# Attention between two sequences on one core: the steady batches and the last batch put in another order

## The chip, the cores and the metric

The kernel runs on one core of a Trainium2 chip. The metric is the device time of one execution, in microseconds (us); less is better. Five engines work side by side and wait for each other by semaphores: TensorE (PE) multiplies matrices into PSUM, VectorE (DVE) and ScalarE (ACT) read PSUM and the on-chip memory, GpSimd (POOL) works on the on-chip memory alone, SyncE (SP) starts transfers. Each engine runs its own instructions in their order.

## The reference

`x` and `y` (`ctx_2048`) are 32 batches of 256 x 1024 floats. `C` is 256 channels, `N` is 1024 columns.

```python
x_q = jnp.einsum('oc,bcn->bno', w_qk, y)
x_k = jnp.einsum('oc,bcn->bon', w_qk, x)
x_v = jnp.einsum('oc,bcn->bon', w_v, x) + b_v[None, :, None]
energy = jnp.einsum('bnc,bcm->bnm', x_q, x_k)
attention = jax.nn.softmax(energy, axis=-1)
attention = attention / (1e-07 + attention.sum(axis=1, keepdims=True))
x_r = jnp.einsum('bcn,bnm->bcm', x_v, attention)
x_r = jax.nn.relu(jnp.einsum('oc,bcn->bon', w_t, x - x_r) + b_t[None, :, None])
return x + x_r
```

So the softmax goes over the rows of the energy, and each column of the result is then divided by its own sum over the rows plus 1e-7 (`EPS`).

## The kernel before

Weights are multiplied together once at the start (`w_qk` with itself, `w_v` with `w_t`, `w_t` alone), and each float operand is split into three forms, HIGH, REST and LOW, so that three quick matmuls add up to one exact product. Six matmuls (three forms, two halves of the channels) make one result of 128 x 512.

Work goes batch by batch, `cur` being the batch in hand, `nxt` the next and `last` the one before. The 1024 rows of the energy are eight row tiles `n` of 128, the columns two halves `h` of 512, the channels two halves `c` of 128. PSUM is `banks`, eight banks used as four pairs. Pairs 0 and 1 hold the energy of two row tiles in turn (`place(n)`), and also the keys and one group of the values; pairs 2 and 3 collect the attention's result for `c` 0 and 1, and before that take the other group of values and the straight part.

The steps of a batch, by method name:

- `values(q)`: 24 matmuls with 256 columns for one group q of four row tiles; then `high` (ACT), `low` and `rest` (DVE) write its three forms. `v0`, `v1` are the two groups.
- `energy(n)`: 12 matmuls. `lowest(n)` (DVE), `exp(n)` (ACT, also the row sum), `recip(n)` (DVE). `high(n, h)` (ACT), `rest(n, h)` (DVE), `scaled(n)` (ACT) and `low(n)` (POOL) write the forms of the softmax, all four of them being `forms(n)`. `share(n)` (DVE, a step for each half) adds the row tile into `acc`, from which the column sums come.
- `straight(c)`: 12 matmuls of `w_t` with x; `straight_out(c)` (ACT) takes it from PSUM to `xe`.
- `attention(n)`: 12 matmuls into pairs 2 and 3, four pieces (c, h) of three.
- `keys(i)`: 12 matmuls for the next batch, with `high` (ACT), `low`, `rest` (DVE) as `k0`, `k1`.
- `columns()` and `inverse()` (DVE): sum `acc` over its rows and spread the reciprocals over the partitions as `rc`. `divided(c)` (DVE) reads pair 2 + c, `joined(c)` (POOL) adds `xe`, and in the next batch `relu(c)` (ACT) and `put(c)` (POOL add of x loaded again by `load_out`, then the store) finish it.
- In the last batch, `finish(c, h)` does the end by quarters: divided, a maximum, a sum, a store.

Every compute engine is wrapped in `InOrder`, so the order of its instructions is that of the calls in the program; the SP queue is ordered by the scheduler. Raw tiles of x and y share four buffers (`rawp`), the softmax forms three (`ep`). Every recorded instruction has the line of the wrapper, L66, so the profile's groups are told apart by tile names: `ef` forms of the softmax, `uf` of the values, `gf` of the keys, `xf`, `yf` of x and y, `nm`, `rs`, `ri` the smallest value of a row, the row sum and its reciprocal.

In a steady batch PE's order is values(0), energy(0), values(1), straight(0), energy(1), straight(1), energy(2), attention(0), energy(3), attention(1) and so on to energy(7), attention(5), then keys(0), attention(6), keys(1), attention(7). In the last batch there are no keys, and the pieces of attention are drawn from a list, three behind each energy:

```python
if n + 2 < NT:
    cur.energy(n + 2)
    attend(3)
```

Of the kernel before, what the change touches and what calls it, by code (L numbers as in the profile page):

```python
# [9 lines left out]
F32 = mybir.dt.float32  # L10
F32R = mybir.dt.float32r
AF = mybir.ActivationFunctionType
ALU = mybir.AluOpType
# [4 lines left out]
def kernel(  # L18
# [24 lines left out]
    FORMS = 3  # L43
    HIGH, LOW, REST = range(FORMS)
# [27 lines left out]
    load = nc.sync.dma_start  # L72
# [3 lines left out]
    def pair(j):  # L76
        return banks[:, 2 * j : 2 * j + 2]
# [4 lines left out]
    def value(v):  # L82
        return v.bitcast(F32)
# [56 lines left out]
    class Weights:  # L140
# [12 lines left out]
        def low(self):  # L153
            act.mul(self.l, self.d, UP)
# [49 lines left out]
    class Batch:  # L204
# [136 lines left out]
        def scaled(self, n):  # L341
            act.mul(self.ef[n][:, LOW], value(self.ef[n][:, HIGH]), 1.0 / UP)

        def low(self, n):
            f = self.ef[n]
            pool.tensor_tensor(f[:, LOW], value(f[:, LOW]), value(f[:, REST]), ALU.add)

        def share(self, n, halves=range(MH)):
            p, ri = self.place(n), self.row[n]
            if n == 0:  # L350
# [36 lines left out]
        def inverse(self):  # L387

            def moved(out_, in_):
                dve.tensor_reduce(out_, in_.unsqueeze(2), AX.X, ALU.add)  # L390

            s = sc[:, :, 0]
            for a in range(1, NG):
                moved(parts[:G32, :, a], parts[ts(a, G32), :, 0])
            dve.tensor_reduce(s[:G32], parts[:G32], AX.X, ALU.add)
            dve.reciprocal(s[:G32], s[:G32])
            moved(s[G32 : 2 * G32], s[:G32])
            moved(s[2 * G32 :], s[: 2 * G32])
            rc = one.tile([P, NB, G32], F32, tag="rc", name=f"rc_{self.b}")
# [23 lines left out]
        def end_sum(self, c):  # L423
            pool.tensor_tensor(self.xo[c], self.xo[c], self.xe[:, c], ALU.add)

        def end_least(self, c):
            act.mul(self.xe[:, c], self.xe[:, c], -1.0)

        def finish(self, c, h):

            if c == 0 and h == 0:
                self.z = one.tile([P, KC, N], F32, tag="z", name=f"z_{self.b}")
            at = ts(h, MB)
            p, zh, xh = pair(2 + c)[:, h], self.z[:, c, at], self.xo[c][:, at]
            final = (c, h) == (KC - 1, MH - 1)
            dve.scalar_tensor_tensor(p, p, ubias[:, c], self.rc[:, at], ALU.add, ALU.mult)
            dve.tensor_tensor(zh, p, self.xe[:, c, at], ALU.max)
            (dve if final else pool).tensor_tensor(zh, zh, xh, ALU.add)
            load(out[self.b, ts(c, P), at], zh)


    def square(into, left, right):
# [86 lines left out]
    for b in range(B - 1):  # L529
        nxt = Batch(b + 1)  # L530

        if b == 0:
            v0 = cur.values(0)
            v0.high()
            v1 = cur.values(1)
            v0.low()
            v0.rest()
            act.copy(th, wtT)
            pool.tensor_tensor(wd, wtT, value(th), ALU.subtract)
            pool.tensor_tensor(  # L540
                product, wt, bv.unsqueeze(1).to_broadcast([P, KC, C]), ALU.mult
            )
# [24 lines left out]
            for h in range(MH):  # L567
                cur.high(1, h)
                cur.rest(1, h)
            cur.straight_out(1)  # L570
            cur.scaled(1)
            cur.low(1)
        else:
            v0 = cur.values(0)
            v0.high()
            cur.energy(0)
            cur.lowest(0)
            v0.low()
# [24 lines left out]
            cur.scaled(1)  # L603
            cur.low(1)
        nxt.load_x()
        cur.energy(2)
        cur.share(1)
        for n in range(2, NT):
# [5 lines left out]
            cur.exp(n)  # L614
            cur.recip(n)
            cur.forms(n)
            cur.attention(n - 2, first_order if b + n == 2 else None)
            if n == 2:
                nxt.x_high(0)
                nxt.x_rest(0)  # L620
# [28 lines left out]
        for q in later:  # L649
# [10 lines left out]
        for c in range(KC):  # L660
            cur.divided(c)
            cur.joined(c)
        for q in later:
            ys[q].low()
        last, cur = cur, nxt


    units = [(n, c, h) for n in range(NT - 2) for c in range(KC) for h in range(MH)]

    def attend(count):  # L670
        for _ in range(count):
            n, c, h = units.pop(0)
            cur.attention(n, [(c, h)])

    v0 = cur.values(0)
    v0.high()
    cur.energy(0)
    cur.lowest(0)
    v0.low()
    v1 = cur.values(1)  # L680
    cur.exp(0)
    cur.recip(0)
    v1.high()
    v0.rest()
    cur.forms(0)
    cur.straight(0)
    cur.straight_out(0)
    last.relu(0)
    last.load_out()
    last.put(0)  # L690
    cur.share(0)
    v1.low()
    cur.energy(1)
    cur.lowest(1)
    v1.rest()
    cur.straight(1)
    cur.energy(2)
    cur.exp(1)
    cur.straight_out(1, ts(0, 1))
    cur.recip(1)  # L700
    more_ef = one.tile([P, KC, FORMS, N], F32R, tag="xf", name="more_ef")
    for n in (3, 4):
        cur.ef[n] = more_ef[:, n - 3]
    for n in range(1, NT):
        if n > 1:
            cur.exp(n)
            cur.recip(n)
        cur.high(n, 0)
        cur.share(n, [1])
        cur.rest(n, 0)  # L710
        if n == 1:
            cur.straight_out(1, ts(1, 1))
        if n + 1 < NT:
            cur.lowest(n + 1)
        cur.high(n, 1)
        cur.share(n, [0])
        cur.rest(n, 1)
        if n + 2 < NT:
            cur.energy(n + 2)
            attend(3)  # L720
        cur.scaled(n)
        cur.low(n)
        if n == 2:
            last.relu(1)
            last.put(1)
            cur.load_out()
        elif n == 4:
            cur.end_sum(0)
        elif n == 5:
            cur.end_sum(1)  # L730
    attend(len(units))
    cur.columns()
    cur.inverse()
    for c in range(KC):
        cur.end_least(c)
    for c in range(KC):
        for h in range(MH):
            for n in (NT - 2, NT - 1):
                cur.attention(n, [(c, h)])
            cur.finish(c, h)  # L740


# [28 lines left out]
```

## Time and profile before

| | |
|---|---|
| median of 3 runs | 1949.26 us (1946.62 to 1949.41) |
| profiled execution, its own time | 1947.41 us |
| its span | 1945.6 us |
| granted TensorE clock | 0.999 |
| busy: PE, DVE, ACT, POOL | 1936.5, 1555.5, 1465.2, 1257.6 us |

The span is what the trace covers, from the first to the last instruction; the execution's own time has 1.8 us more around it. In a row of the timeline stand start, duration, engine, line, operation, output<-input, shape and count, and in brackets idle time ahead of it with what ended it.

### The profile page before, as it was taken

Reading aid. Unit: us, or ns where it says so; the run is one execution under the profiler, and the core shown is the slowest. Engines: PE = TensorE matmul, PEld = TensorE weight load, DVE = VectorE, ACT = ScalarE, POOL = GpSimd, SP = SyncE. Lnnn points to the kernel's source line nnn. Section 1 sums busy time; section 2 is a strip of 40 time slices with the busy share of each in tenths; the row PEclk is TensorE's granted clock in tenths of the full one; section 3 lists DMA queues with packets and bytes.
Section 4 is the critical chain, followed back from the end, with each engine's and each line's share of the span. In section 5 each row is a group of like instructions: output and inputs, shape, how many; then the busy total and the mean of one; then the engine's idle time right before and its main releaser. Section 6 shows DMA issues by size and latency. Waiting matters only on the chain.

```text
span 1945.6 us, 25143 instructions
## 1 busy us (share of the span) xinstructions
PE 1936.5 (100%) x9246; PEld 1631.4 (84%) x9246; DVE 1555.5 (80%) x2162; ACT 1465.2 (75%) x1899; POOL 1257.6 (65%) x646
## 2 busy tenths in 40 slices
PE   9999999999999999999999999999999999999998
PEld 8888888888888888888888888888888888888886
DVE  7877788877888778887788877788777888778888
ACT  7777777777777877777877777777777777777765
POOL 5666766667657676666666666666667566676565
PEclk9999999999999999999999999999999999999999
DMA  4644546545455444555454644546445455454531
GB/s 138 152 113 118 124 111 141 123 116 130 108 130 130 120 119 113 126 132 124 113 123 116 145 114 119 119 119 141 114 118 125 110 141 123 115 131 109 130 98 44
DMA packets 81852, 235.35 MB, mean 121 GB/s; under 512 B 7488, under 2 KB 8384, under 8 KB 81728
## 3 DMA queue, kind: packets, MB, share of 16 engines
q0 software_dynamic: 35136, 98.58, 29.3%
q1 hardware_dynamic: 46448, 135.02, 20.5%
q8 instruction: 73, 1.20, 0.2%
q14 instruction: 51, 0.42, 0.1%
q10 hardware_dynamic: 144, 0.13, 0.0%
HBM read 134.61 MB, written 33.55 MB: 86 GB/s over the span
## 4 chain that ended last, share of the span: by engine, by line
PE 99%; DVE 1%; issue 0%; ACT 0%; DVEq 0%; ACTq 0%
PE banks L66 99%; DVE z L66 0%; DVE banks L66 0%; DVE nm L66 0%; DVE ef L66 0%; DVE acc L66 0%; DVE parts L66 0%; DVE rc L66 0%; DVE sc L66 0%; ACT ef L66 0%; DVE few L66 0%; DVE ri L66 0%; DVEq L66 0%; ACTq L66 0%
## 5 line engine op out<-in xcount | busy, mean ns | idle before, releaser
L66 POOL TENSOR_TENSOR ef<-ef 128x1024 fp32r<-128x1024 f32 x254 | 611.4, 2407 | 444.8 <-ACT ef L66 328.4
L66 PE MATMUL banks<-gf,yf 128*128 128x512 f32 x3072 | 739.4, 390 | 2.2 <-DVE acc L66 2.1
L66 PE MATMUL banks<-ef,uf 128*128 128x512 f32 x3048 | 731.9, 389 | 0.0
L66 PEld LDWEIGHTS banks<-gf,yf 128*128 128x128 f32 x3072 | 574.0, 188 | 122.5 <-issue 4.8
L66 PEld LDWEIGHTS banks<-ef,uf 128*128 128x128 f32 x3048 | 572.1, 188 | 118.8
L66 DVE SCALAR_TENSOR_TENSOR ef<-banks,ri,ef 128x512 fp32r<-128x512 f32 x508 | 358.4, 746 | 210.4 <-ACT ef L66 210.3
L66 ACT ACTIVATE banks<-banks,nm 128x1024 f32<-128x1024 f32 x256 | 278.0, 1086 | 275.8 <-DVE nm L66 269.8
L66 DVE TENSOR_REDUCE nm<-banks 128x1 f32<-128x1024 f32 x256 | 312.8, 1222 | 86.6 <-PE banks L66 84.9
L66 ACT ACTIVATE ef<-banks,ri 128x512 fp32r<-128x512 f32 x508 | 322.6, 687 | 54.6 <-DVE ri L66 45.3
L66 DVE SCALAR_TENSOR_TENSOR acc<-banks,ri,acc 128x512 f32<-128x512 f32 x448 | 314.3, 742 | 0.2
L66 ACT ACTIVATE ef<-ef 128x1024 fp32r<-128x1024 f32 x254 | 270.5, 1065 | 7.1
L66 POOL DMA_DIRECT2D yf<-in_ctx_dram x63 | 76.7, 1217 | 189.5 <-ACT yf L66 187.4
L66 PEld LDWEIGHTS banks<-vw,xf 128*128 128x128 f32 x1536 | 192.6, 191 | 4.9
L66 PE MATMUL banks<-vw,xf 128*128 128x256 f32 x1536 | 194.1, 283 | 0.0
L66 PE MATMUL banks<-xf,tw 128*128 128x512 f32 x768 | 185.2, 390 | 0.0
L66 PE MATMUL banks<-xf,gw 128*128 128x512 f32 x768 | 184.7, 389 | 0.0
L66 PEld LDWEIGHTS banks<-xf,gw 128*128 128x128 f32 x768 | 144.0, 188 | 29.9
L66 PEld LDWEIGHTS banks<-xf,tw 128*128 128x128 f32 x768 | 142.2, 188 | 28.2
L66 POOL TENSOR_TENSOR z<-z,xe 128x1024 f32<-128x1024 f32 x62 | 147.5, 2394 | 22.1 <-DVE z L66 22.1
L66 POOL TENSOR_TENSOR z<-z,xo 128x1024 f32<-128x1024 f32 (+1 forms) x65 | 152.1, 2340 | 3.7 <-DVE z L66 3.7
L66 POOL TENSOR_TENSOR xf<-x,xf 128x1024 fp32r<-128x1024 f32 x62 | 149.3, 2407 | 0.0
L66 ACT ACTIVATE yf<-yf 128x1024 fp32r<-128x1024 f32 x127 | 131.0, 1055 | 2.0
(72 smaller groups left out, 1314.2 us busy)
## 6 DMA issues: line engine op xcount, KB each, us to landing
x<-in_x_dram SPq DMA_DIRECT2D x64, 512.0 KB, 3.5
y<-in_ctx_dram SPq DMA_DIRECT2D x64, 512.0 KB, 4.6
xo<-in_x_dram SPq DMA_DIRECT2D x64, 512.0 KB, 3.5
yf<-in_ctx_dram POOLq DMA_DIRECT2D x63, 512.0 KB, 6.5
yf<-yf POOLq DMA_DIRECT2D x63, 512.0 KB, 5.2
xf<-xf POOLq DMA_DIRECT2D x62, 512.0 KB, 6.2
out_dram<-z SPq DMA_DIRECT2D x62, 512.0 KB, 3.0
out_dram<-z SPq DMA_DIRECT2D x4, 256.0 KB, 2.0
```

Source lines behind the costliest of these rows:

```text
L66: self.last = getattr(self.engine, name)(*args, **kwargs)
```

## The change

Four things are changed.

1. Steady batches. PE does values(0) and values(1) one behind the other, then energy(0), straight(0), energy(1), straight(1), energy(2); straight(1) goes into pair 2. On DVE the two steps of v0 and the first of v1 stand ahead of lowest(0), share(0) stands behind lowest(1). `relu(0)`, `load_out` and `put(0)` of the batch before go behind the forms of row tile 1. `attention(0)` starts with the pieces of c = 1.
2. The end of a steady batch. `divided(0)` and `joined(0)` stand ahead of k1's `low` and `rest`, `divided(1)` and `joined(1)` behind them.
3. The last batch (with the steps of the batch before that are still open) is a list of words, each one step, with halves of energies and pieces of attention as single words. The last row tile's forms are made from a copy on ACT (`end_share`, `end_high`, `end_scaled`) and two steps on POOL (`end_rest` for the first half, `low` by halves).
4. Its column sums. `EPS / P` is added in the first share; a matmul with `few`, now a matrix that adds the four groups of 32 rows (`gather_groups`, filled by POOL in batch 0), and one reciprocal stand where `inverse` had eight small steps. The first quarter of the end is divided into `z` and done by POOL and ACT.

```diff
     def share(self, n, halves=range(MH)):
...
-                    dve.tensor_scalar(a, p[:, h], ri, None, ALU.mult)
+                    if self.b < B - 1:
+                        dve.tensor_scalar(a, p[:, h], ri, None, ALU.mult)
+                    else:
+                        dve.tensor_scalar(a, p[:, h], ri, EPS / P, ALU.mult, ALU.add)
...
+        def end_group_sums(self):
+            into = self.place(NT - 2)[:, 0, :NB]
+            pe.matmul(into, few, parts[:, :, 0], start=True, stop=True)
+
+        def end_recip(self):
+            dve.reciprocal(sc[:, :, 0], self.place(NT - 2)[:, 0, :NB])
...
+        def end_share(self, h):
+            act.mul(self.sh[:, ts(h, MB)], self.place(n)[:, h], self.row[n])
+        def end_high(self, h):
+            act.copy(self.ef[n][:, HIGH, ts(h, MB)], self.sh[:, ts(h, MB)])
+        def end_scaled(self, h):
+            act.mul(f[:, LOW], value(f[:, HIGH]), 1.0 / UP)
+        def end_rest(self, h):
+            pool.tensor_tensor(f[:, REST], self.sh[:, ts(h, MB)], value(f[:, HIGH]), ALU.subtract)
...
+    def gather_groups():
+        two_groups = 2 * G32
+        pool.tensor_tensor(
+            few[:, :two_groups], ident[:, :two_groups], ident[:, two_groups:], ALU.add
+        )
+        pool.tensor_tensor(few[:, :G32], few[:, :G32], few[:, G32:two_groups], ALU.add)
+        for a in range(1, NG):
+            pool.tensor_copy(few[:, ts(a, G32)], few[:, :G32])
...
             v0 = cur.values(0)
             v0.high()
+            v1 = cur.values(1)
+            v0.low()
+            v0.rest()
             cur.energy(0)
+            v1.high()
+            v1.low()
             cur.lowest(0)
-            v0.low()
-            v1 = cur.values(1)
+            v1.rest()
+            cur.straight(0)
             cur.exp(0)
             cur.recip(0)
-            v1.high()
-            v0.rest()
-            cur.forms(0)
-            cur.straight(0)
+            cur.high(0, 0)
+            cur.rest(0, 0)
+            cur.high(0, 1)
+            cur.rest(0, 1)
             cur.straight_out(0)
-            last.relu(0)
-            last.load_out()
-            last.put(0)
-            cur.share(0)
-            v1.low()
+            cur.scaled(0)
+            cur.low(0)
             cur.energy(1)
             cur.lowest(1)
-            v1.rest()
+            cur.share(0)
             cur.exp(1)
             cur.recip(1)
-            cur.straight(1)
-            cur.straight_out(1, ts(0, 1))
+            cur.straight(1, 2)
+            last.load_out()
...
-            cur.straight_out(1, ts(1, 1))
+            cur.straight_out(1)
             cur.scaled(1)
             cur.low(1)
+            last.relu(0)
+            last.put(0)
...
-        k1.low()
-        k1.rest()
         cur.attention(NT - 1)
...
+        if nxt.b < B - 1:
+            divide(0)
+            k1.low()
+            k1.rest()
+            divide(1)
...
+    steps = """
+        V0 vh0 ylow klow krest div0 vl0 E01 join0 vr0 pos0 E00 min0 exp0 div1 V1 E11 ri0 sum01
+        vh1 h00 outx E10 vl1 h01 X0 join1 min1 exp1 lastx r01 xw0 s0 r00 sum00 ri1 put0 sum10
+        sum11 E21 h10 E20 min2 X1 r10 h11 r11 exp2 ri2 sum21 x11 h21 l0 sum20 E30 s1 E31 r21 l1
+        h20 min3 r20 A011 E41 vr1 x10 A010 exp3 ri3 E40 sum31 min4 s2 l2 A001 h30 A110 h31 r31
+        A101 r30 exp4 ri4 h40 A111 h41 E51 A210 sum30 sum40 E50 s3 xs01 pos1 r40 r41 E60 sum41
+        E61 A000 s4 min5 A201 exp5 ri5 h51 min6 A100 h50 A200 xsw1 r51 sum51 sum50 l3 A310 A300
+        exp6 E71 s5 l4 ri6 put1 h61 r50 E70 h60 r61 l5 r60 s6 min7 A211 sum61 A400 sum60 exp7
+        ri7 sh0 sum71 A410 A301 sum70 A311 eh0 sh1 A500 l6 es0 eh1 cols es1 A510 A610 er0 el0
+        A401 A501 r71 G A600 least01 A700 A710 A411 A601 inv el1 leastw1 turn d00 plus relu A701
+        d10 m10 o10 o00 d01 m01 A511 o01 A611 A711 d11 m11 o11
+    """
```

The words: V values (the digit is q), E energy (n, h), X straight (c), A attention (n, c, h), G the group matmul; vh, vl, vr high, low and rest of the values; min, exp, ri, sum (n, h), h, r, s, l the steps of a row tile; sh, eh, es, er, el the same for the last one; x, xw straight_out; cols, inv, turn the column sums, the reciprocal and its spread; d, m, o divided, maximum and out by quarters (c, h).

More of the change, by code (lines that the diff above doesn't have):

```diff
@@ L342, in scaled, with low @@
             act.mul(self.ef[n][:, LOW], value(self.ef[n][:, HIGH]), 1.0 / UP)
-        def low(self, n):
-            f = self.ef[n]
+        def low(self, n, at=slice(0, None)):
+            f = self.ef[n][:, :, at]
             pool.tensor_tensor(f[:, LOW], value(f[:, LOW]), value(f[:, REST]), ALU.add)
@@ L349, in share @@
             p, ri = self.place(n), self.row[n]
-            if n == 0:
+            if not hasattr(self, "acc"):
                 self.acc = one.tile([P, N], F32, tag="acc", name=f"acc_{self.b}")
@@ L398, in inverse, with turned @@
             moved(s[2 * G32 :], s[: 2 * G32])
+            self.turned()
+        def turned(self):
             rc = one.tile([P, NB, G32], F32, tag="rc", name=f"rc_{self.b}")
@@ L421, in put, with end_sum, end_least @@
             load(out[self.b, ts(c, P)], self.z[:, c])
[L423 to L431, printed above, removed]
+        def end_sum(self, c, at=slice(0, None)):
+            xo = self.xo[c][:, at]
+            pool.tensor_tensor(xo, xo, self.xe[:, c, at], ALU.add)
+        def end_least(self, c, at=slice(0, None)):
+            act.mul(self.xe[:, c, at], self.xe[:, c, at], -1.0)
@@ new lines, in end_share @@
+        def end_share(self, h):
+            n = NT - 1
+            if h == 0:
+                self.sh = rawp.tile([P, N], F32, tag="raw", name="share")
+            act.mul(self.sh[:, ts(h, MB)], self.place(n)[:, h], self.row[n])
+        def end_high(self, h):
+            n = NT - 1
+            if n not in self.ef:
+                self.ef[n] = ep.tile([P, FORMS, N], F32R, tag="ef", name="ef_last")
+            act.copy(self.ef[n][:, HIGH, ts(h, MB)], self.sh[:, ts(h, MB)])
+        def end_scaled(self, h):
+            f = self.ef[NT - 1][:, :, ts(h, MB)]
+            act.mul(f[:, LOW], value(f[:, HIGH]), 1.0 / UP)
@@ L432, in finish, with piece @@
+        def end_rest(self, h):
+            f = self.ef[NT - 1][:, :, ts(h, MB)]
+            pool.tensor_tensor(f[:, REST], self.sh[:, ts(h, MB)], value(f[:, HIGH]), ALU.subtract)
+        def piece(self, c, h):
+            if not hasattr(self, "z"):
                 self.z = one.tile([P, KC, N], F32, tag="z", name=f"z_{self.b}")
             at = ts(h, MB)
-            p, zh, xh = pair(2 + c)[:, h], self.z[:, c, at], self.xo[c][:, at]
-            final = (c, h) == (KC - 1, MH - 1)
-            dve.scalar_tensor_tensor(p, p, ubias[:, c], self.rc[:, at], ALU.add, ALU.mult)
@@ L437, in finish, with end_divided @@
-            dve.tensor_tensor(zh, p, self.xe[:, c, at], ALU.max)
-            (dve if final else pool).tensor_tensor(zh, zh, xh, ALU.add)
-            load(out[self.b, ts(c, P), at], zh)
+            return pair(2 + c)[:, h], self.z[:, c, at], self.xe[:, c, at], self.xo[c][:, at]
+        def end_divided(self, c, h):
+            p, zh, xe, xh = self.piece(c, h)
+            dve.scalar_tensor_tensor(
+                p if c + h else zh, p, ubias[:, c], self.rc[:, ts(h, MB)], ALU.add, ALU.mult
+            )
@@ new lines, in end_max, with end_plus, end_relu, end_out @@
+        def end_max(self, c, h):
+            p, zh, least, xh = self.piece(c, h)
+            dve.tensor_tensor(p if c == h == 1 else zh, p, least, ALU.max)
+        def end_plus(self):
+            p, zh, xe, xh = self.piece(0, 0)
+            pool.tensor_tensor(zh, zh, xe, ALU.add)
+        def end_relu(self):
+            zh = self.piece(0, 0)[1]
+            act.activation(zh, zh, AF.Relu)
+        def end_out(self, c, h):
+            p, zh, xe, xh = self.piece(c, h)
+            if c == h == 1:
+                dve.tensor_tensor(zh, p, xh, ALU.add)
+            else:
+                pool.tensor_tensor(zh, zh, xh, ALU.add)
+            load(out[self.b, ts(c, P), ts(h, MB)], zh)
@@ L616 @@
             cur.forms(n)
-            cur.attention(n - 2, first_order if b + n == 2 else None)
+            cur.attention(n - 2, first_order if n == 2 else None)
+            if b == 0 and n == 4:
+                gather_groups()
             if n == 2:
@@ L656, with divide @@
             ys[q].scaled()
-        k1.low()
-        k1.rest()
         cur.attention(NT - 1)
-        for c in range(KC):
+        def divide(c):
             cur.divided(c)
             cur.joined(c)
-        for q in later:
-            ys[q].low()
-        last, cur = cur, nxt
[L668 to L740, printed above, removed]
+        if nxt.b < B - 1:
[3 more added lines that the diff above has]
+            divide(1)
+            for q in later:
+                ys[q].low()
+        last, cur = cur, nxt
+    v = {}
+    def open_values(q):
+        v[q] = cur.values(q)
@@ new lines, in late_high @@
+    def late_high(n, h):
+        if n == 3 and n not in cur.ef:
+            more = one.tile([P, KC, FORMS, N], F32R, tag="xf", name="more_ef")
+            cur.ef[n], cur.ef[n + 1] = more[:, 0], more[:, 1]
+        cur.high(n, h)
+    steps = {
+        "klow": lambda: k1.low(),
+        "krest": lambda: k1.rest(),
+        "ylow": lambda: ys[B * MH - 1].low(),
+        "div": lambda c: last.divided(c),
+        "join": lambda c: last.joined(c),
+        "pos": lambda c: last.relu(c),
+        "lastx": lambda: last.load_out(),
+        "put": lambda c: last.put(c),
+        "V": open_values,
+        "vh": lambda q: v[q].high(),
+        "vl": lambda q: v[q].low(),
+        "vr": lambda q: v[q].rest(),
+        "X": lambda c: cur.straight(c),
+        "xw": lambda c: cur.straight_out(c),
+        "x": lambda c, h: cur.straight_out(c, ts(h, 1)),
+        "E": lambda n, h: cur.energy(n, [h]),
+        "min": lambda n: cur.lowest(n),
+        "exp": lambda n: cur.exp(n),
+        "ri": lambda n: cur.recip(n),
+        "sum": lambda n, h: cur.share(n, [h]),
+        "h": late_high,
+        "r": lambda n, h: cur.rest(n, h),
+        "s": lambda n: cur.scaled(n),
+        "l": lambda n: cur.low(n),
+        "A": lambda n, c, h: cur.attention(n, [(c, h)]),
+        "outx": lambda: cur.load_out(),
+        "xsw": lambda c: cur.end_sum(c),
+        "xs": lambda c, h: cur.end_sum(c, ts(h, MB)),
+        "leastw": lambda c: cur.end_least(c),
+        "least": lambda c, h: cur.end_least(c, ts(h, MB)),
+        "sh": lambda h: cur.end_share(h),
+        "eh": lambda h: cur.end_high(h),
+        "es": lambda h: cur.end_scaled(h),
+        "er": lambda h: cur.end_rest(h),
+        "el": lambda h: cur.low(NT - 1, ts(h, MB)),
+        "cols": lambda: cur.columns(),
+        "G": lambda: cur.end_group_sums(),
+        "inv": lambda: cur.end_recip(),
+        "turn": lambda: cur.turned(),
+        "d": lambda c, h: cur.end_divided(c, h),
+        "m": lambda c, h: cur.end_max(c, h),
+        "plus": lambda: cur.end_plus(),
+        "relu": lambda: cur.end_relu(),
+        "o": lambda c, h: cur.end_out(c, h),
+    }
@@ L744 @@
+    """
+    for word in STEPS.split():
+        name = word.rstrip("0123456789")
+        steps[name](*(int(a) for a in word[len(name):]))
 _INS = [
```

2 lines of the change are left out of this document (added).

## The prediction

> **What bounds the kernel now.** First the page: which engine fills the span, at what clock, and what the chain of work that ended last is made of.
>
> ```profile
> span 1945.6 us, 25143 instructions
> ...
> PE 1936.5 (100%) x9246; PEld 1631.4 (84%) x9246; DVE 1555.5 (80%) x2162; ACT 1465.2 (75%) x1899; POOL 1257.6 (65%) x646
> ...
> PEclk9999999999999999999999999999999999999999
> ...
> PE 99%; DVE 1%; issue 0%; ACT 0%; DVEq 0%; ACTq 0%
> ```
>
> PE is busy throughout and carries 99% of the chain, at an even clock. As the ends of matmuls are modelled, I look at starts instead, in the timeline of PE alone around the head of a steady batch.
>
> ```profile
> 975.29 2.88 PE L66 MATMUL banks<-ef,uf 128*128 128x512 f32 x12
> 978.01 3.04 PE L66 MATMUL banks<-vw,xf 128*128 128x256 f32 x24
> 980.89 2.91 PE L66 MATMUL banks<-gf,yf 128*128 128x512 f32 x12
> 983.63 3.04 PE L66 MATMUL banks<-vw,xf 128*128 128x256 f32 x24
> 986.51 2.91 PE L66 MATMUL banks<-xf,tw 128*128 128x512 f32 x12
> 989.25 2.88 PE L66 MATMUL banks<-gf,yf 128*128 128x512 f32 x12
> 994.69 2.88 PE L66 MATMUL banks<-gf,yf 128*128 128x512 f32 x12
> ```
>
> Twelve matmuls of 512 columns take 2.72 us from start to start (975.29 to 978.01; 989.25 to 994.69 is two blocks), 0.2267 each; the 24 of a group of values take 2.88. Nothing waits: a steady batch is pure PE work, and no order of other engines' work can shorten it. The only excess is 0.02 us in the block behind each group of values (980.89 to 983.63 and 986.51 to 989.25 are 2.74). So a gain has to come from the last batch, and a loss could come from any wait that the new steady order opens, thirty times over.
>
> The last batch, in the timeline from its first matmul on:
>
> ```profile
> 1881.28 3.04 PE L66 MATMUL banks<-vw,xf 128*128 128x256 f32 x24
> ...
> 1897.96 2.88 PE L66 MATMUL banks<-gf,yf 128*128 128x512 f32 x12
> 1900.88 1.23 DVE L66 TENSOR_REDUCE nm<-banks 128x1 f32<-128x1024 f32 x1 [0.95 <-PE banks L66]
> ...
> 1902.91 3.00 PE L66 MATMUL banks<-gf,yf 128*128 128x512 f32 x12 [2.07 <-DVE acc L66]
> 1905.74 2.20 PE L66 MATMUL banks<-ef,uf 128*128 128x512 f32 x9
> 1905.94 1.22 DVE L66 TENSOR_REDUCE nm<-banks 128x1 f32<-128x1024 f32 x1 [0.47 <-PE banks L66]
> ...
> 1907.09 0.74 DVE L66 SCALAR_TENSOR_TENSOR acc<-banks,ri,acc 128x512 f32<-128x512 f32 x1
> ...
> 1907.97 3.00 PE L66 MATMUL banks<-gf,yf 128*128 128x512 f32 x12
> ...
> 1923.16 2.99 PE L66 MATMUL banks<-gf,yf 128*128 128x512 f32 x12
> ...
> 1931.42 8.32 PE L66 MATMUL banks<-ef,uf 128*128 128x512 f32 x36
> ...
> 1940.41 0.75 DVE L66 SCALAR_TENSOR_TENSOR banks<-banks,ubias,rc 128x512 f32<-128x512 f32 x1
> 1941.19 0.69 DVE L66 TENSOR_TENSOR z<-banks,xe 128x512 f32<-128x512 f32 x1
> 1941.99 0.69 DVE L66 TENSOR_TENSOR z<-z,xo 128x512 f32<-128x512 f32 x1
> ```
>
> Here PE does wait. The last 36 matmuls need 36 x 0.2267 = 8.16, so PE is through at 1939.58, 58.30 us after 1881.28. Its work: up to the end of energy(2) 1897.96 + 2.72 - 1881.28 = 19.40; five more energies 13.60; eight attentions, 96 matmuls, 21.76; together 54.76. The waits are 58.30 - 54.76 = **3.54 us**: 2.23 ahead of energy(3) (1902.91 - 1900.68), which needs the first row tile of that place to be read out; about 0.30 in each of four rounds of energy and nine attention matmuls, (1923.16 - 1902.91) / 4 = 5.06 against 21 x 0.2267 = 4.76; 0.1 at the end. The 0.30 is seen in one round: energy(3) ends at 1905.63, lowest(3) starts at 1905.94, the share of tile 2 at 1907.09 lasts 0.74, and energy(4) starts at 1907.97. That is 2.34 us on DVE, covered by 9 x 0.2267 = 2.04 of PE.
>
> **Part one, the steady batches.** PE's work per batch is the same; one of two changes from values to another block goes: 30 x 0.02 = **0.6 us**. What must hold is that nothing comes late. I go through the new order on the times of the batch above (V0 is values(0) at 978.01), with these rows of DVE, ACT, SP and again ACT (and one of the groups by form, for the low and rest of the values):
>
> ```profile
> 976.61 1.25 DVE L66 STREAM_TRANSPOSE rc<-sc 128x1024 f32<-128x1024 f32 x1
> 977.78 1.18 DVE L66 SCALAR_TENSOR_TENSOR gf<-gf,banks 128x1024 fp32r<-128x1024 f32 x1
> 979.00 1.23 DVE L66 SCALAR_TENSOR_TENSOR gf<-banks,gf 128x1024 fp32r<-128x1024 f32 x1
> 980.14 2.47 DVE L66 SCALAR_TENSOR_TENSOR z<-banks,ubias,rc 128x1024 f32<-128x1024 f32 x2
> 989.67 1.40 DVE L66 TENSOR_SCALAR acc<-banks,ri 128x512 f32<-128x512 f32 x2
> ...
> L66 DVE SCALAR_TENSOR_TENSOR uf<-banks,uf 128x1024 fp32r<-128x1024 f32 x64 | 77.4, 1210 | 0.0
> ...
> 981.09 1.03 ACT L66 ACTIVATE uf<-banks 128x1024 fp32r<-128x1024 f32 x1 [0.65 <-PE banks L66]
> ...
> 995.26 13.65 SPq L167 DMA_DIRECT2D y<-in_ctx_dram  x2
> ...
> 1031.18 1.04 ACT L66 CAST yf<-y 128x1024 fp32r<-128x1024 f32 x1
> ```
>
> - V1 is now due at 978.01 + 2.88 = 980.89 and overwrites pair 2, so divided(0) must have read it. divided(0) takes the place of k1.low at 977.78 and, at 1.27 (two take 2.47), ends at 979.05: 1.8 us to spare. The two steps of k1 end at about 981.4; energy(0), which needs them, is due at 978.01 + 5.76 = 983.77. divided(1) ends at 982.6, straight(0), which overwrites pair 3, is due at 986.5.
> - v0.high ends at 982.1 as before; v0.low and v0.rest, 1.21 each, follow divided(1) and end at 985.0, energy(1) is due at 989.2. v1.high ends at 985.0, v1.low at 986.2, lowest(0) at 987.9, v1.rest at 989.1; straight(1), now into pair 2, is due at 991.95.
> - energy(2) is due at 994.67 and needs share(0), which stands behind lowest(1) now. From energy(1)'s end at 991.95: 0.2 to start, 1.15, to the next step, and 0.74 for the first half make 994.05 (the 1.15 and 0.74 are those of 1905.94 and 1907.09 above); the second half, 0.66 later as 1.40 for two has it, is needed 1.36 later. Spare 0.6, the narrowest place.
> - Of the moved steps, put(0) goes some 8 us later on POOL; its store on SP goes with it to about 1003, and the load of y behind it, issued at 995.26, waits as long. That y is first read at 1031.18: free. The order of loads and stores on SP is the same in both programs. The five small POOL steps that fill `few` lie in batch 0, ahead of two DMAs whose data the keys need only after four more blocks of 2.72: free; without that cover they cost what they last, once.
>
> So part one: -0.6, with bounds 0 and -0.6.
>
> **Part two, the last batch.** The list is laid out so that the rows above do not bind. Each place is refilled behind more PE work: between E20's end and E30 stands straight(1), 2.72; between E31 and E40 stand A011, E41 and A010, 0.68 + 1.36 + 0.68 = 2.72; between E40 and E51 stand four pieces, 2.72; all against the 2.34 that the round above needs. energy(2) has straight(0) in front of it; E60 needs tile 4's steps, which stand ahead of lowest(5) on DVE; E71 has 4.08 of pieces in front of it (from E61's end) for lowest 1.15, a rest and a share, 0.7 each. So the 3.54 should go: **-3.54**. If the 2.34 grew by 0.4 on DVE, these would wait again (a rival below). POOL has 13 steps of at most 2.41 us in the 42 us before energy(7) ends (54.8 less the nineteen pieces behind it, 12.9), 31 of 42, and stays off PE's way; its mean is in the page:
>
> ```profile
> L66 POOL TENSOR_TENSOR ef<-ef 128x1024 fp32r<-128x1024 f32 x254 | 611.4, 2407 | 444.8 <-ACT ef L66 328.4
> ```
>
>
> The end is the second place where something could come late. Two rows of DVE for it from the same timeline, then four groups of the list by form (busy us, mean ns):
>
> ```profile
> 1928.88 0.76 DVE L66 SCALAR_TENSOR_TENSOR acc<-banks,ri,acc 128x512 f32<-128x512 f32 x1
> ...
> 1931.65 1.24 DVE L66 TRANSPOSE_TENSOR_REDUCE parts<-acc 128x32 f32<-128x1024 f32 x1
> ...
> L66 ACT ACTIVATE ef<-banks,ri 128x512 fp32r<-128x512 f32 x508 | 322.6, 687 | 54.6 <-DVE ri L66 45.3 <-POOL ef L66 9.0
> ...
> L66 POOL TENSOR_TENSOR z<-z,xo 128x512 f32<-128x512 f32 x3 | 3.8, 1283 | 3.7 <-DVE z L66 3.7
> ...
> L66 PE MATMUL banks<-few 128*128 128x128 f32 x10 | 2.5, 437 | 1.1 <-DVE few L66 1.1
> ...
> L66 DVE RECIPROCAL sc<-sc 32x32 f32<-32x32 f32 x32 | 10.9, 341 | 1.1
> ```
>
> From energy(7)'s end (1925.88) to the first share of tile 7 (1928.88) it was 3.0 us; two shares, 1.4, and the column sums, 1.24, make 5.7. The group matmul stands behind ten pieces, 6.8 us: 1.1 to spare, and this matmul and one reciprocal stand where `inverse` had eight small steps of DVE. Behind it: the reciprocal (at most 0.34), the transpose 1.25, divided 0.75 twice and a maximum 0.69, with lags some 4.2, against six pieces, 4.08. They run level, and the three pieces behind (2.04) cover the 1.44 of the next divided and maximum. ACT and POOL bring the last row tile's forms: two ACT steps, 0.69 each, and two POOL steps of half size, 1.28 each, make 6.9 with the 3.0 ahead of them, due after 7.9. So PE sets the end, and the saving on DVE is worth nothing by itself.
>
> After PE's last matmul come three DVE steps in both kernels. Before, they began at 1940.41, though the matmul's modelled end is 1931.42 + 8.32 = 1939.74; a free DVE begins 0.04 behind such an end (1897.96 + 2.88 = 1900.84, and 1900.88). So 0.67 - 0.04 = **-0.63** goes there.
>
> The group matmul itself is new on PE. The five matmuls with `few` show ten records, two each, 437 ns busy. Two in sequence are 0.87, the upper bound; below, it cannot cost less than nothing, since PE must do it. I take 0.4, half of that, since those ten stand in the cold start of the kernel and move 128 columns, this one 32: **+0.4**. The Trainium skill, "FP8 and Floating Point Precision", TensorE Precision Notes, says that true FP32 takes four passes through the array; the trace shows two records for each such matmul. Four passes of that length are an estimated 1.75 and would leave a gain of 3.0.
>
> **The sum.** -3.54 - 0.63 + 0.4 - 0.6 = **-4.37 us**. The profiled execution took 1947.41 (span 1945.6 and 1.8 around it) and would take 1943.0; the three runs shown have their median at 1949.26, so I forecast **1944.9**. The runs lie between 1946.62 and 1949.41, so 0.2% (3.9 us) is about what a measurement can tell from no change, and the forecast is hardly more than that.
>
> **Rivals.**
> - *The handovers keep waiting.* With ACT and DVE both reading the same bank, or POOL late, some 0.3 stays at five of the new handovers: 1.5, so 1946.4. For it: the spare is only 0.4 at three of them. Against: the 2.34 they are held to is already a measured chain.
> - *The matmul is dear and the change of block costs nothing to begin with.* At 0.87 for the matmul and 0.3 for the values, the gain is 3.6: 1945.7. For it: 0.02 is the size of the trace's grain. Against: the steady batch is 60.2 us throughout, with that 0.02 in it.
> - *Slower: V1 waits for divided(0) in each steady batch.* It now follows V0 directly. If divided(0) ran where it did (980.14 + 1.27, and 0.14 until PE goes on, as from 1907.83 to 1907.97 above), V1 would wait 0.66 us, thirty times: 20 us, 1964.9. It decides from divided(0) ending after 980.75. For it: DVE is on the edge there, with the inverse ending just as V0 starts. Against: k1's two steps are moved behind, 1.8 to spare.
> - *The group matmul runs four records.* The rows give two for a matmul with `few`, but of another size; at four of 437 ns it takes 1.75, PE and with it the end come 1.35 later than forecast: 1946.3. The skill's sentence on four passes speaks for it, the ten records of five matmuls against it.
>
> **How the numbers follow.** Forecast 0.52, of which 0.37 beyond 0.2% and 0.15 within, as run to run differences of a us or more either side decide there; handovers 0.20 (0.05 and 0.15); dear matmul 0.13 (0.08 and 0.05); four records 0.08 (0.02 and 0.06); V1 0.07 (0.02 within, 0.05 slower). Sum: faster 0.52, same 0.43, slower 0.05. The range goes from 1942.6 (the forecast less 2.3, as far as the lowest run lies under the median) to 1947.4 (the handover case and 1 us); what is left out is V1's 0.07 and about 0.1 at the ends.
>
> **What would show it.** In the profile after: values x48 in one row of PE, followed by one block of 2.74, and a batch of 60.18 us; 54.8 to 55.3 us from the last batch's first matmul to its last with no idle time put down to DVE; two records of the group matmul; the last divided right behind the last matmul. It would be wrong if PE idles ahead of V1 or of energy(2) in every batch, or if the end is a chain of DVE from the transpose on.

## The result, and the profile after

The changed kernel took 1942.97 us (median of 11 runs, 1942.0 to 1943.72) against 1948.2 of the kernel before (11 runs, 1946.62 to 1949.41): a ratio of 0.9974, interval 0.9966 to 0.9982. The forecast was 1944.9, faster, with hardly more than 0.2%. The profiled execution took 1943.16 where that of before took 1947.41, and its span is 1941.4.

PE around the head of the steady batch that starts at 978 us, from the timeline (start, duration, count at the end):

```profile
978.28 5.92 PE L66 MATMUL banks<-vw,xf 128*128 128x256 f32 x48
984.03 2.91 PE L66 MATMUL banks<-gf,yf 128*128 128x512 f32 x12
986.78 2.88 PE L66 MATMUL banks<-xf,tw 128*128 128x512 f32 x12
989.50 2.88 PE L66 MATMUL banks<-gf,yf 128*128 128x512 f32 x12
```

Values take 5.75 us in one row, the block behind them 2.75, the next ones 2.72. Between the first values of two steady batches lie 60.18 us in place of 60.20. DVE in the same stretch:

```profile
976.87 1.25 DVE L66 STREAM_TRANSPOSE rc<-sc 128x1024 f32<-128x1024 f32 x1
978.32 1.28 DVE L66 SCALAR_TENSOR_TENSOR z<-banks,ubias,rc 128x1024 f32<-128x1024 f32 x1 [0.20 <-DVE rc L66]
...
992.42 1.22 DVE L66 TENSOR_REDUCE nm<-banks 128x1 f32<-128x1024 f32 x1 [0.56 <-PE banks L66]
993.56 1.40 DVE L66 TENSOR_SCALAR acc<-banks,ri 128x512 f32<-128x512 f32 x2
```

divided(0) ends at 979.60, 1.56 us before values(1) begins at 978.28 + 2.88 = 981.16; the first half of share(0) ends at about 994.3, energy(2) starts at 994.94. Both have the room that was worked out, less 0.2 for divided(0), which waits for the transpose (k1's step in that place did not need it).

The last batch on PE, with DVE's last steps:

```profile
1880.97 3.04 PE L66 MATMUL banks<-vw,xf 128*128 128x256 f32 x24
...
1900.38 2.88 PE L66 MATMUL banks<-gf,yf 128*128 128x512 f32 x12
1903.10 0.84 PE L66 MATMUL banks<-ef,uf 128*128 128x512 f32 x3
1903.78 1.52 PE L66 MATMUL banks<-gf,yf 128*128 128x512 f32 x6
1905.14 0.84 PE L66 MATMUL banks<-ef,uf 128*128 128x512 f32 x3
1905.82 1.52 PE L66 MATMUL banks<-gf,yf 128*128 128x512 f32 x6
...
1929.62 0.31 PE L66 MATMUL banks<-parts,few 128*128 128x32 f32 x2
1929.75 0.94 PE L66 MATMUL banks<-ef,uf 128*128 128x512 f32 x3
1930.53 1.55 PE L66 MATMUL banks<-ef_last,uf 128*128 128x512 f32 x6
1931.92 0.85 PE L66 MATMUL banks<-more_ef,uf 128*128 128x512 f32 x3
...
1935.32 0.84 PE L66 MATMUL banks<-ef_last,uf 128*128 128x512 f32 x3
```

```profile
1930.36 1.25 DVE L66 STREAM_TRANSPOSE rc<-sc 128x1024 f32<-128x1024 f32 x1
...
1934.16 0.76 DVE L66 SCALAR_TENSOR_TENSOR banks<-banks,ubias,rc 128x512 f32<-128x512 f32 x1 [0.26 <-PE banks L66]
...
1936.20 0.76 DVE L66 SCALAR_TENSOR_TENSOR banks<-banks,ubias,rc 128x512 f32<-128x512 f32 x1 [0.56 <-PE banks L66]
1936.99 0.70 DVE L66 TENSOR_TENSOR banks<-banks,xe 128x512 f32<-128x512 f32 x1
1937.73 0.69 DVE L66 TENSOR_TENSOR z<-banks,xo 128x512 f32<-128x512 f32 x1
```

No idle time stands at any row of PE. Its work ends at 1935.32 + 0.68 = 1936.00, 55.03 us after 1880.97, where before it took 58.30. The last three DVE steps begin 0.20 us behind that, where before it was 0.83 (1940.41 against 1939.58), and DVE now waits for PE in the last two quarters. The chain that ended last and PE's waits over the whole span say the same:

```profile
14 pieces in order of time: start us, us, what
...
7.38 0.14 issue
7.52 1928.66 PE banks L66 x9230
1936.18 0.03 issue
1936.20 0.77 DVE banks L66
```

```profile
PE banks L66 <- DVE parts L66: 1.1, 1, 1.1
PE banks L66 <- DMA stage<-in_L_xattn_w_t_dram: 0.9, 1, 0.9
```

One piece of PE, 1928.66 us long, with three DVE steps behind it. The two waits left lie in the first 8 us; the second, for a load, put the first values at 15.24 us, where they were at 14.70 before.

### The profile page after: what moved, and what is told of

The parts are those of the page before. It is cut to its first block, busy times and chain, and to the rows that moved or that the text cites. A ratio compares the mean times of both kernels' runs of the same rounds, so it can differ in the third digit from the quotient of the medians.

```text
span 1941.4 us, 25177 instructions
## 1 busy us (share of the span) xinstructions
PE 1934.2 (100%) x9248; PEld 1632.0 (84%) x9248; DVE 1558.5 (80%) x2154; ACT 1463.1 (75%) x1873; POOL 1261.1 (65%) x654
## 4 chain that ended last, share of the span: by engine, by line
PE 99%; DMA 0%; DVE 0%; SPq 0%; issue 0%
PE banks L66 99%; DMA stage<-in_L_xattn_w_t_dram 0%; DVE banks L66 0%; DVE z L66 0%; SPq L113 0%; SPq L106 0%
## 5 line engine op out<-in xcount | busy, mean ns | idle before, releaser
L66 PEld LDWEIGHTS banks<-vw,xf 128*128 128x128 f32 x1536 | 188.7, 192 | 2.6
L66 PE MATMUL banks<-vw,xf 128*128 128x256 f32 x1536 | 189.5, 283 | 0.0
L66 POOL TENSOR_TENSOR z<-z,xe 128x1024 f32<-128x1024 f32 (+1 forms) x63 | 163.8, 2817 | 4.8 <-DVE z L66 4.8
```

The source lines that it names most:

```text
L66: self.last = getattr(self.engine, name)(*args, **kwargs)
```

## The experiments

**The last batch alone.** The steady batches of before with the new list:

```diff
             v0 = cur.values(0)
             v0.high()
-            v1 = cur.values(1)
-            v0.low()
-            v0.rest()
             cur.energy(0)
-            v1.high()
-            v1.low()
             cur.lowest(0)
+            v0.low()
+            v1 = cur.values(1)
...
-            divide(0)
             k1.low()
             k1.rest()
+            divide(0)
             divide(1)
```

> The steady batches of the kernel before with the list of the changed kernel for the last batch. Theory: a steady batch takes 60.20 us, the last one 55.0 us from its first matmul to the end of its last, and DVE starts its last divided 0.2 us behind PE; 3.9 us less than before (3.27 of PE time and 0.63 at the end). Rival (steady order worth more): 3.0 us less or under that.

Measured: 1943.31 us (1942.69 to 1944.2) against 1947.54, ratio 0.9977 (0.9967 to 0.9986). The trace has 60.20 us a batch, and the last batch on PE takes 55.03, from its first matmul to the end of its last (1935.44 + 0.68 - 1881.09):

```profile
1881.09 3.04 PE L66 MATMUL banks<-vw,xf 128*128 128x256 f32 x24
...
1935.44 0.84 PE L66 MATMUL banks<-ef_last,uf 128*128 128x512 f32 x3
```

Nearly the whole gain is the last batch's.

**The steady batches alone**, in two forms. The first left the last batch of before as it was, but put divided(0) ahead of k1 in front of it too.

```diff
-        k1.low()
-        k1.rest()
         cur.attention(NT - 1)
+        cur.divided(0)
+        cur.joined(0)
+        k1.low()
+        k1.rest()
+        cur.divided(1)
+        cur.joined(1)
```

> The steady batches of the changed kernel with the last batch of the kernel before. Theory (the gain lies in the last batch): a steady batch takes 60.18 us in place of 60.20, the last batch keeps 58.3 us from its first matmul to the end of its last, with 2.2 us of wait ahead of energy(3); about 0.6 us less than before in all, 0.03%, not to be told from no change by the times. Rival (the steady order itself is worth more than the 0.6, since the medians moved by 5.2 us and the two profiled spans by 4.2): 1.5 us or more less than before.

Measured: 1948.69 against 1947.54, ratio 1.0004 (0.9996 to 1.0013). A batch does take 60.18 us, but the edit made a wait of its own: the old last batch does energy(0) straight behind values(0), and its keys now come late.

```profile
1879.62 3.03 PE L66 MATMUL banks<-vw,xf 128*128 128x256 f32 x24
1883.47 0.70 PE L66 MATMUL banks<-gf,yf 128*128 128x512 f32 x2 [0.82 <-DVE gf L66]
```

From values(0) to energy(0) it is 3.85 us in place of 2.88: some 1.0 us is lost here, more than the 0.6 that was to be seen. The two places of the change belong together: divided(0) can go first only where the two groups of values stand side by side. The second form kept k1 first in front of the last batch alone (shown against the first form).

```diff
+        if nxt.b == B - 1:
+            k1.low()
+            k1.rest()
         cur.divided(0)
         cur.joined(0)
-        k1.low()
-        k1.rest()
+        if nxt.b < B - 1:
+            k1.low()
+            k1.rest()
```

> As the first steady-only kernel, but the low and rest of k1 ahead of both divided in front of the last batch, so that energy(0) of the last batch, there directly behind values(0), finds its keys as in the kernel before. Theory: 60.18 us a batch, 58.3 us of PE in the last batch where the clock holds and 59.8 where it falls, 0.6 to 0.9 us less than the kernel before. Rival (the steady order costs something the batch period does not show): the same time as the kernel before, or more.

Measured: 1946.65 against 1948.23, ratio 0.9992 (0.9983 to 1.0001); span 1944.9, with 60.18 us a batch and 58.33 on PE in the last, first values at 14.69. Against the profile of before (14.70 and 1945.6) the span is 0.7 us shorter. That is the 0.6 and the greater part of a single 0.27: in every profile with the old steady order (four of them) one row tile of the 23rd batch costs PE 0.24 to 0.28 us, behind one DVE step that starts 0.35 late; with the new steady order PE loses 0.05 there or nothing. Why that step is late stays open.

**The slower rival as a kernel.** The changed kernel with k1 ahead of divided(0) in the steady batches:

```diff
-            divide(0)
             k1.low()
             k1.rest()
+            divide(0)
             divide(1)
```

> The changed kernel, but with the low and rest of k1 ahead of divided(0) at the end of the steady batches again, values still side by side. The slower rival of the prediction as an experiment: divided(0) then ends about 0.55 us after values(1) is due in pair 2; with 0.14 us until PE goes on, values(1) waits 0.66 to 0.7 us in each of the 29 or 30 steady batches: a batch of 60.84 us and 20 us more than the changed kernel (1963 us). If something else hid it (PE's queue, a later start of PE that gives it back), the batch stays at 60.18 us.

Measured: 1962.74 us, 60.85 us a batch.

```profile
987.73 3.03 PE L66 MATMUL banks<-vw,xf 128*128 128x256 f32 x24
991.19 3.13 PE L66 MATMUL banks<-vw,xf 128*128 128x256 f32 x24 [0.42 <-DVE z L66]
```

values(1) starts 3.46 us behind values(0) in place of 2.88. One execution is 20 us longer than the changed kernel's median, as the rival had it. Its mechanism is real; the order of three DVE steps is what keeps it away.

**The narrowest place.** share(0) with its halves swapped:

```diff
-            cur.share(0)
+            cur.share(0, [1, 0])
```

> The changed kernel, in the steady batches share(0) does its second half first. Tests the narrowest place of the steady order: the first half of energy(2) then waits for the second step of share(0). By the rows of the changed kernel that ends at 994.96, PE goes on 0.14 later, at 995.10, where it now starts at 994.94: 0.16 us a batch, 60.34, and 4.8 us more in all (1948). Rival (the place has more slack than that): 60.18.

Measured: 1950.65 us, 60.47 us a batch: 0.29 us a batch, not 0.16.

```profile
995.38 2.88 PE L66 MATMUL banks<-xf,tw 128*128 128x512 f32 x12
998.27 3.00 PE L66 MATMUL banks<-gf,yf 128*128 128x512 f32 x12
1001.11 2.20 PE L66 MATMUL banks<-ef,uf 128*128 128x512 f32 x9
```

energy(2) was due at 998.10 and starts at 998.27, 0.17 late, where the rows gave 0.16. But the block then takes 2.84 to the next start, 0.12 more than 2.72: after the wait the matmuls come slower at first (the second starts 0.31 behind the first in this trace, not 0.23). So this wait costs PE itself and 0.12 us. The last batch of the kernel before has the same: the block behind each wait takes 2.82 to 2.84 there (1902.91 to 1905.74 in the lines of the prediction is one).

**Less cover at two handovers of the last batch.**

```diff
-  A011 E41 vr1 x10 A010 exp3 ri3 E40 sum31
+  A011 E41 vr1 x10 exp3 ri3 E40 A010 sum31
-  A101 r30 exp4 ri4 h40 A111 h41 E51 A210
+  r30 exp4 ri4 h40 h41 E51 A101 A111 A210
```

> The changed kernel, in the last batch with less PE work at two handovers: A010 stands behind E40, A101 and A111 behind E51, so that 2.04 us of PE work stand between E31 and E40 and between E40 and E51, as in the rounds of the kernel before. Theory (2.34 us of DVE and lags must be covered): PE waits 0.3 us at each, 0.6 us in the last batch's PE time, 55.6 in place of 55.0. Rival (the waits of before came from the order on ACT and DVE, not from the cover): 55.0 again.

Measured: 55.67 us on PE in the last batch, 0.64 more than 55.03. Time 1943.61 (one run).

```profile
1903.55 3.11 PE L66 MATMUL banks<-gf,yf 128*128 128x512 f32 x12
1906.49 2.22 PE L66 MATMUL banks<-ef,uf 128*128 128x512 f32 x9
1908.78 1.67 PE L66 MATMUL banks<-gf,yf 128*128 128x512 f32 x6
```

The two half energies take 2.94 in place of 2.72, the nine attention matmuls 2.29 to the next start in place of 2.04, and the next half energy 1.51 in place of 1.36. That is 0.22 at the first handover and 0.40 at the second, where 0.3 was expected at each. The order on ACT and DVE is untouched, so the rival falls: with 2.04 of cover the wait is back, with 2.72 it is gone, and the cover decides. The limit lies between these two.

**The column sums as before, in the new list.**

```diff
-        "inv": lambda: cur.end_recip(),
+        "inv": lambda: cur.inverse(),
...
-  er0 el0 A401 A501 r71 G A600
+  er0 el0 A401 A501 r71 A600
```

> The changed kernel with the column sums of the last batch done as before: no group matmul on PE, EPS added as a fifth column, eight small steps of DVE where the one reciprocal stands. Forecast's theory (PE sets the end, the saving on DVE is worth nothing by itself): the last batch's PE work falls by the 0.27 us that the matmul cost, the end with it. Rival (the DVE chain becomes the end): the transpose starts 1.1 us later, the divided, maximum and sum behind it run one behind the other and the end is 0.3 us or more later.

Measured: 1943.4 us (1943.06 to 1944.69), ratio 0.9976 (0.9966 to 0.9985). PE's last batch falls to 54.76, by the 0.27 of the matmul, and its end comes at 1934.78 in this trace. DVE's does not:

```profile
1930.45 1.25 DVE L66 STREAM_TRANSPOSE rc<-sc 128x1024 f32<-128x1024 f32 x1
1931.78 0.75 DVE L66 SCALAR_TENSOR_TENSOR z<-banks,ubias,rc 128x512 f32<-128x512 f32 x1
1932.45 0.75 DVE L66 SCALAR_TENSOR_TENSOR banks<-banks,ubias,rc 128x512 f32<-128x512 f32 x1
...
1935.31 0.75 DVE L66 SCALAR_TENSOR_TENSOR banks<-banks,ubias,rc 128x512 f32<-128x512 f32 x1
```

From the transpose on DVE runs without a wait and is the end. Its values began at 1880.02 and its span ends at 1941.43, 61.41 us later; in the changed kernel it is 1941.38 - 1880.97 = 60.41. So the group matmul costs PE 0.27 and, with that paid, brings the end 1.0 us earlier. The two medians, 0.43 apart, were not taken side by side and don't settle its size; the 1.0 is that of two traces, one execution each.

**The kernel before once more**, because its times spread more than the two profiles explain.

> The kernel before once more, for a second profile of it. Theory: 60.20 us a batch, 58.3 us for the last batch's PE work, and the difference to the first profile lies in the start (the first values began at 14.70 us in the profile before and at 15.24 in the one after, behind a load) and in single waits such as the 0.27 us of one batch. Rival: the waits of the last batch differ by 1 us or more from run to run, and that is why the medians moved by more than the two profiled runs.

Measured: 1948.68 us, span 1946.9, and 59.83 us of PE in the last batch, 1.5 more than in the first profile. Neither theory had the reason. It is in the windows view (PE busy (count), the same for PEld, DVE, ACT, POOL, then the granted clock, DMA share, GB/s):

```profile
1895.00:1902.80 7.80, 5.73 (x26) 4.48 (x25) 6.38 (x9) 5.51 (x8) 2.83 (x2) 1.00 0.17 67
1902.90:1906.20 3.30, 3.30 (x9) 2.52 (x9) 1.87 (x4) 2.94 (x6) 2.38 (x1) 0.50 0.01 2
1906.30:1930.00 23.70, 23.59 (x101) 18.33 (x101) 19.15 (x28) 16.31 (x23) 16.68 (x7) 1.00 0.06 23
```

```profile
1897.68 2.88 PE L66 MATMUL banks<-gf,yf 128*128 128x512 f32 x12
1902.63 4.57 PE L66 MATMUL banks<-gf,yf 128*128 128x512 f32 x12 [2.07 <-DVE acc L66]
1907.05 2.20 PE L66 MATMUL banks<-ef,uf 128*128 128x512 f32 x9
```

After the wait ahead of energy(3) the granted clock is 0.50 for the window, and twelve matmuls take 4.42 us to the next start in place of 2.83. In the first profile the same wait left the clock at full speed:

```profile
1902.90:1906.20 3.30, 3.29 (x15) 2.71 (x15) 2.40 (x5) 2.94 (x6) 2.42 (x1) 1.00 0.01 2
```

The first steady-only run above shows the fall as well, the second does not. What sets the two cases apart can be read from the traces. In each of the eleven, the times at which the granted clock changes lie whole multiples of 3.413 us apart: here 5.03, 1902.84, 1906.26 and 1943.80, which is 556, 1 and 11 of them. Laid over the wait, this grid has all 2.23 us of idle time within one stretch of 3.413 in the two traces with the fall. In the two without, it cuts the wait in two: 0.32 and 1.91 us in the first profile, 1.11 and 1.12 in the second steady-only run. So in these four traces the clock falls where one stretch holds 2.23 us of idle time and not where it holds 1.91, and which of the two happens depends on where the grid lies in that execution. The Trainium skill, "TensorE: Matmul & The Clock Gate", Part 1, has a free-running window of 3413 ns whose idleness halves the clock, and names an idle time of about 3.4 us. The traces agree with the window and its length, but here 2.23 us of idle time within one were enough.

**The gap filled.** To see whether that is what the medians moved by, beyond the profiles:

```diff
     cur.energy(2)
+    for i in range(9):
+        matmul(pair(2)[:, 0], cur.xf[:, HIGH, 0, :P], cur.xf[:, HIGH, 0, :MB], True, True)
     cur.exp(1)
```

> The kernel before with nine matmuls added behind energy(2) of the last batch, into pair 2, which attention(0) overwrites: 9 x 0.2267 = 2.04 us of PE work in the 2.23 us in which PE waited ahead of energy(3); nothing else is moved, and the result is the same. Theory (a wait of 2.2 us lets the granted clock fall to 0.5 for 3.41 us in some executions, as in the second profile of the kernel before, and this makes up for what the medians moved beyond the 4.2 us of the two first profiles): no 0.43 us spacing behind energy(3) any more, the last batch stays at 58.3 us, the times lose their upper part and the median falls by 0.5 to 1.5 us though PE does more. Rival (the clock fell there by chance, or the spread comes from the loads at the start alone): median and spread as before, 0 +- 0.5.

Measured: 1947.77 us (1946.83 to 1948.38) against 1948.25 (1947.42 to 1950.14), ratio 0.9998 (0.9989 to 1.0007), 58.25 us on PE in the last batch.

```profile
1897.42 2.88 PE L66 MATMUL banks<-gf,yf 128*128 128x512 f32 x12
1900.14 2.20 PE L66 MATMUL banks<-xf 128*128 128x512 f32 x9
1902.37 2.99 PE L66 MATMUL banks<-gf,yf 128*128 128x512 f32 x12
```

The upper part of the times is gone, as the theory has it: none of 11 runs above 1948.4, against 5 of 20 above 1949. The mean granted clock of the single runs, which is on record too, says it more plainly. It is 0.998 in both profiles with the fall and 0.999 in the first profile, without it. It is 0.998 or lower in 8 of the 20 runs of the kernel before that were taken beside this one, and in 17 of its 55 runs beside three sets of experiments, but in none of the 11 with the gap filled, and in none of the 30 runs of the changed, the last-batch and the column-sum kernel, which have no such wait. So the wait brings the fall. What that does to the median is not shown: its 0.48 lies inside the interval and just short of the theory's 0.5 to 1.5, and two of the five runs above 1949 stand at 0.999.

## Why the prediction was right

The terms on the two first profiles, as spans, in us:

| term | forecast | measured |
|---|---|---|
| waits of the last batch on PE | -3.54 | -3.54 (58.30 to 55.03, with the matmul's 0.27 taken out) |
| group matmul | +0.4 | +0.27 |
| end behind PE's last matmul | -0.63 | -0.63 (0.83 to 0.20) |
| change of block, 30 batches | -0.6 | -0.6 (60.20 to 60.18) |
| single wait of the 23rd batch | none | -0.27 |
| start | none | +0.54 (14.70 to 15.24) |
| sum | -4.37 | -4.23; the spans differ by 4.2 |

The sum comes closer than its parts. The 0.13 by which the matmul was cheaper, the -0.27 and the +0.54 were not forecast and nearly cancel, and that is luck. The start is that of single executions: in the eleven profiles the first values begin between 13.86 and 15.24 us, whatever the order of the steps.

The forecast of the time itself, 1944.9, was 1.93 us too high. Of this, 1.06 is its base, a median of three runs (1949.26) where eleven gave 1948.2, and 0.86 is a gain of 5.23 in place of 4.37. The time lies only 0.37 above the lower end of the range. That end was set 2.3 under the forecast "as far as the lowest run lies under the median"; by the runs shown this distance is 2.64.

- *The bound and the place of the gain* held: PE carried the span, the steady batches gave 0.02 each, the rest came from the last batch, and the last-batch kernel shows it by itself.
- *The handovers* held. Their rival did not come: no wait of 0.3 is left anywhere in the last batch. But the prediction took each 0.30 for waiting alone. By the starts in that timeline, nine matmuls take 2.23 in place of 2.04 and the energy behind them 2.82 to 2.84 in place of 2.72: 0.19 is the wait, 0.10 to 0.12 the slower block behind it. So the chain to be covered was 2.23 from start to start in that round (1905.74 to 1907.97), and not 2.34.
- *The slower rival* did not come, and was a real danger: 20 us, had three steps of DVE kept their order. The room of 1.8 was 1.56.
- *The matmul* has two records of PE, 0.13 us from its first to the next matmul, and 0.13 more in the nine behind it (1929.75 to 1931.92 is 2.17 against 2.04). Those nine lose as much as a block behind a wait does; whether for the same reason no run shows. Four records, the rival that went with the Trainium skill's sentence on true FP32, are not what the trace shows for this form.
- *"The saving on DVE is worth nothing by itself"* was wrong. The prediction set the free DVE at the end (-0.63) and the saved steps apart as if the first did not need the second. Without the group matmul the transposed reciprocals come 1.0 us later and DVE is the end again. The chain had been found to "run level" with PE; a chain that runs level has no 1 us to give. The saved small steps of `inverse` are seven, not eight, in the trace: 1.83 us from 1928.62 to the transpose at 1930.45 in the column-sum kernel, where the reciprocal takes 0.40 (1929.96 to 1930.36) in the changed one.
- *The times* moved by 5.2 us, the two profiled executions by 4.25. The prediction called the clock even, from one profile, and took the spread of before as mere spread. A part of it is the half clock behind the 2.2 us wait: 1.5 us in the executions that have it, and the two profiles compared here are both without it. At 17 of 55 runs this is some 0.5 us on average; with the 0.54 of the late start in the profile after, this estimate covers the 0.98 that the two differences are apart, but it rests on single profiles. The changed kernel has no such wait, and its runs lie within 1.7 us. The row that asked for this was shown, the wait of 2.07 ahead of energy(3), and the question whether the clock outlasts it was not put.

## What to carry to other kernels

Where PE is full from start to start in the loop, look for the time at its ends: count the matmuls of the last batch, take them from the time between its first and last start, and what remains is to be had. For each buffer that is used in turn, compare the chain that empties it (here about 2.2 us) with the PE work that stands between its two uses, and move work there until it covers. Take a second profile of a kernel whose times spread more than the forecast gain; one execution may not show the half clock that a wait brings to others.

## What the runs showed of the hardware

- An idle time of PE of 2.23 us brought the granted clock to 0.5 for 3.41 us in some executions and not in others of one kernel; 1.5 us each time. The clock fell in the two traces in which all of it lay within one stretch of a grid of 3.413 us, and not in the two in which the grid cut it (at most 1.91 us in one stretch).
- After a wait, a block of twelve matmuls takes 0.10 to 0.12 us more (2.84 in place of 2.72 in the swapped-halves kernel, 2.82 to 2.84 in the last batch before, at full clock).
- A matmul of float operands with 32 columns among others cost PE 0.27 us, half of it in the matmuls behind it (the changed kernel against the column-sum kernel).
